# A graph network with attention and experts in one kernel: half PSUM tiles in a pool of their own, layer 2's alphas turned into one tile, and attention's first norms moved into the graph layers

## The chip, the cores and the metric

The kernel runs on one NeuronCore of a Trainium2 chip. A core has a matrix engine (TensorE, "PE" in the profile; its weight loads are "PEld"), a vector engine (VectorE, "DVE"), an activation engine (ScalarE, "ACT"), a general engine (GpSimd, "POOL") and a queue engine (SyncE, "SP") that here only issues DMAs. PE writes into PSUM, a memory of eight banks; DVE and ACT read it from there. Each engine works through its own list of instructions in order, and waits for other engines by semaphores. The metric is the device time of one execution in microseconds (us); lower is better.

## The reference

There are 625 nodes with 768 features and 20,000 edges, sorted by destination. All is float32. Cut to what matters:

```python
y = layernorm(x)
# two graph attention layers over the edges and the self loops
def gat(x, W, a_src, a_dst, bias, heads):
    xl = x @ W                                   # per head
    alpha_src, alpha_dst = xl . a_src, xl . a_dst
    e = leaky_relu(alpha_src[src] + alpha_dst[dst], 0.2)
    alpha = segment_softmax(e, dst)
    return segment_sum(xl[src] * alpha, dst) + bias
h1 = relu(layer_norm(gat(y, W1, ..., heads=4)) * g1 + be1) + (y @ Wr1 + br1)     # 1024 wide
h  = layer_norm(gat(h1, W2, ..., heads=1)) * g2 + be2 + (h1 @ Wr2 + br2)         # 768 wide
x = x + h
# one transformer block on layernorm(x): 12 heads, causal; then 8 experts, top 1
z = layernorm(x);  n = layernorm(z) * ln1_g + ln1_b
q, k, v = n @ Wq, n @ Wk, n @ Wv
u = z + causal_attention(q, k, v) @ Wp + bp
m = layernorm(u) * ln2_g + ln2_b
e = argmax(m @ Wg)
x = x + u + relu(m @ W1[e] + b1[e]) @ W2[e] + b2[e]
```

## The kernel before

The nodes are cut into five tiles of 125 rows (`T = 5`, `R = 125`), and most of the work is done tile by tile. The kernel has four stages.

**Counts (0 to about 129 us).** The edges become a dense matrix `C` of counts (destination by source) with one-hot matmuls. The counts gather in the PSUM tile `cps`, which is five banks wide (pool `cps`); projections and transposes use three more banks (pool `pps`, tag `p1`). `decode` turns `cps` into `C` with ACT and DVE. A branch follows (`tc.If(ok == 0)`, L445) whose body, rarely run, counts again in `cps`. All engines pass the branch.

**Graph layers (about 129 to 381 us).** A `Messages` object holds a tile's weights: `neg` marks missing edges, `weigh` makes the softmax weights `z` of a head (ACT adds the alphas, L170; DVE the leaky part, L171; DVE the maximum, L490; ACT the exponential, L493; DVE multiplies by `C`, L494), `turn` transposes `z` on PE, and `gather` multiplies it by `xl` into `agg`. PSUM comes from one pool, `gps`, with three tags: `half` (one bank, two buffers; from `psum_half`), `p2` (two banks, two buffers) and `acc` (two banks, one buffer). Halves take the projections and residuals: `project_residual` (L162) and `project` (L577) in layer 1, `second_residual` (L613) in layer 2. Its results are added to `x` on DVE (L615).

At the passage to layer 2, the alphas of the source nodes (`al2`) are turned to rows: for each tile a half tile, a transpose on PE (L624) and a copy on ACT (L625). Then `weigh2` makes the weights of the first three tiles; `messages2(t)` turns the next tile, weighs the one three ahead, gathers, adds the bias `br2` to `x` (L648), and `finish2` scales, normalises (L125 to L137) and adds to `x` (L640). The order on PE is written out by hand in these layers (`tc.manual_schedule`); on DVE and ACT a scheduler places instructions by its own estimates, and `tc.issue_after` holds one behind another. ACT works with tables of functions: going from a square root to an exponential or back takes a table load.

**Attention (about 381 to 640 us).** For each tile, the first norms are made: `bn_stats` (L735), mean and variance into `norms` (L736), two square roots on ACT (L738, L739), a reciprocal (L740), and `h` (L743, L745), which PE transposes (L715) into `hT`. `h` has two buffers. `hT` feeds the projections V (L759), Q and K (L796). `ln1_g` and `ln1_b` come by DMAs from POOL's queue (`load_v`, L685). The heads follow, two at a time.

**Experts (about 640 us to the end).** Rows are sorted to experts and worked off in blocks; expert weights (`ew`) stream in through SP's queue.

SBUF tiles come from pools whose addresses are taken over by later pools, so a tile also waits for the last reader of whatever lay at its place.

Of the kernel before, what the change touches and what calls it, by code (L numbers as in the profile page):

```python
# [9 lines left out]
F32 = mybir.dt.float32  # L10
# [4 lines left out]
AF = mybir.ActivationFunctionType  # L15
OP = mybir.AluOpType
AX = mybir.AxisListType
PSUM = bass.MemoryType.PSUM
DRAM = bass.MemoryType.DRAM

N = 625
R = 125
T = N // R
XR = 120
D = 768
KD = D // 128
# [15 lines left out]
B = 128  # L42
# [14 lines left out]
def row_bcast(v, n):  # L57

    return bass.AP(tensor=v.tensor, offset=v.offset, ap=[[0, B], [1, n]])
# [3 lines left out]
def gnn_moe_kernel(ctx: ExitStack, tc: tile.TileContext, p, out):  # L63
    nc = tc.nc
# [3 lines left out]
    keep = ctx.enter_context(tc.tile_pool(name="keep", bufs=1))  # L68
    small = ctx.enter_context(tc.tile_pool(name="small", bufs=4))
# [8 lines left out]
    x = xid[:, :, :D]  # L78
# [25 lines left out]
    eps = const.tile([128, 1], F32, name="eps")  # L104
# [14 lines left out]
    idr = ident[:R, :R]  # L119
# [14 lines left out]
    def norm_affine(o, a, n, g, b):  # L134
        mu, rs = norm_stats(a, n)
        nc.vector.scalar_tensor_tensor(o, a, mu, g, op0=OP.subtract, op1=OP.mult)
        nc.vector.scalar_tensor_tensor(o, o, rs, b, op0=OP.mult, op1=OP.add)  # L137

    def cols(t):
        return slice(t * R, (t + 1) * R)  # L140


    with tc.tile_pool(name="gnn", bufs=1) as gp:
        C = gp.tile([R, T, N], F32, name="C")
# [30 lines left out]
        with tc.tile_pool(name="oneh", bufs=12) as op_, \  # L175
# [104 lines left out]
            for t in range(2, T):  # L280
                nc.vector.scalar_tensor_tensor(tl, pt0[:R, :G], float(t * R), tl, op0=OP.is_ge,
                                               op1=OP.add)
# [4 lines left out]
                                           dst, op0=OP.mult, op1=OP.add)  # L287
# [157 lines left out]
            with tc.If(ok == 0):  # L445
# [13 lines left out]
                for t in range(T):  # L459

                    nc.vector.tensor_add(C[:, t, cols(t)], C[:, t, cols(t)], idr)

        with tc.tile_pool(name="gw", bufs=2, reuse_waits="tile") as gw, \
                tc.tile_pool(name="gps", bufs=2, space=PSUM, reuse_waits="tile") as ps:

            def psum_half():
                return ps.tile([128, 512], F32, tag="half", name="ph")

            def turn(dst, src, k, t):

                tp = ps.tile([128, 8, 128], F32, tag="p2", name="tp")
                for i in range(k):
                    nc.tensor.transpose(tp[:, i, :R], src[:, i * 128:(i + 1) * 128], idr)
                nc.scalar.copy(dst[:, :, cols(t)], tp[:, :k, :R])

            class Messages:


                def __init__(self, t, heads):
                    self.t, self.heads = t, heads  # L480
                    self.neg = gw.tile([R, N], F32, name="neg")
                    nc.vector.tensor_scalar(self.neg, C[:, t, :], 0.0, NEG, op0=OP.is_equal,
                                            op1=OP.mult)
                    self.tot = small.tile([R, HEADS], F32, name="tot")
                    self.z, self.zT, self.agg = {}, {}, None

                def weigh(self, h, rows, al, z=None):
                    z = z if z is not None else lifted(rows, al, self.t, h)
                    m = small.tile([R, 2], F32, name="m")
                    nc.vector.tensor_tensor_reduce(z, z, self.neg, scale=1.0, scalar=-3.0e38,  # L490
                                                   op0=OP.add, op1=OP.max, accum_out=m[:, 0:1])
                    nc.vector.tensor_scalar_mul(m[:, 1:2], m[:, 0:1], -1.0)
                    nc.scalar.activation(z, z, AF.Exp, bias=m[:, 1:2])  # L493
                    nc.vector.scalar_tensor_tensor(z, z, 1.0, C[:, self.t, :], op0=OP.mult,  # L494
                                                   op1=OP.mult, accum_out=self.tot[:, h:h + 1])
                    self.z[h] = z

                def turn(self, h):
# [37 lines left out]
            msgs = {0: Messages(0, HEADS)}  # L536
# [49 lines left out]
            hw = [messages(0)]  # L586
# [13 lines left out]
                project(t - 1)  # L600
            turn(h1T, hw[T - 1], KH, T - 1)


            b2 = load_bc("bc2", p["L0_gnn_b2"], D)
            g2 = load_bc("bc3", p["L0_gnn_g2"], D)
# [13 lines left out]
            br2 = load_bc("bc1", p["L0_gnn_br2"], D)  # L619
            second_residual(0, (1,))  # L620
            rows2 = gp.tile([R, HEADS, N], F32, tag="rows", name="rows2")
            for t in range(T):
                tp = psum_half()
                nc.tensor.transpose(tp[:R, :R], al2[:, 0, t, 0:1].to_broadcast([R, R]), idr)  # L624
                nc.scalar.copy(rows2[:, 0, cols(t)], tp[:R, :R])  # L625

            def weigh2(t):
                msgs[t] = Messages(t, 1)
# [13 lines left out]
            def messages2(t):  # L642
                if t + 1 < T:
                    msgs[t + 1].turn(0)
                if t + 3 < T:
                    weigh2(t + 3)
                msgs[t].gather(0, [(0, 0, 384), (512, 384, 384)], xl2, "p2" if t % 2 else "acc")
                nc.vector.tensor_add(x[:, t, :], x[:, t, :], br2)  # L648
                finish2(t)

            for t in range(3):
# [16 lines left out]
    nblk = keep.tile([1, 1], I32, name="nblk")  # L668
    table = keep.tile([1, 4, NS + 1], I32, name="table")
    first = keep.tile([1, 1], I32, name="first")  # L670


    sx = ctx.enter_context(tc.tile_pool(name="sx", bufs=1, side="right", reuse_waits="tile"))
    xa = sx.tile([B, D], F32, name="xa")
    xaT = sx.tile([128, KD, B], F32, name="xaT")
    ra = sx.tile([B, D + 1], F32, name="ra")
    pool, SP, PE = mybir.EngineType.Pool, mybir.EngineType.SP, mybir.EngineType.PE
    rt = ctx.enter_context(ExitStack())
    ap = rt.enter_context(tc.tile_pool(name="rt", bufs=1, side="right", reuse_waits="tile"))
    with tc.tile_pool(name="att", bufs=1, reuse_waits="tile") as a1, \  # L680
            tc.tile_pool(name="aw", bufs=3, reuse_waits="tile") as aw, \
            tc.tile_pool(name="aps", bufs=2, space=PSUM, reuse_waits="tile") as ps:

        def load_v(b, v):
            nc.gpsimd.dma_start(b, row_bcast(v, D))  # L685
            return b[:R]

        l1 = a1.tile([B, 2, D], F32, tag="aT", name="l1")
        l1g = load_v(l1[:, 0, :], p["L0_ffn_ln1_g"])
        l1b = load_v(l1[:, 1, :], p["L0_ffn_ln1_b"])  # L690
        bp, l2g, l2b = (load_v(ap.tile([B, D], F32, tag=n, name=n), p["L0_ffn_" + m])
                        for n, m in (("bp", "bp"), ("l2g", "ln2_g"), ("l2b", "ln2_b")))
        wg = ap.tile([128, KD, E], F32, name="wg")
        nc.gpsimd.dma_start(wg, p["L0_ffn_Wg"].rearrange("(k p) e -> p k e", p=128))
# [27 lines left out]

        norms = a1.tile([R, T, 4], F32, name="norms")

        def normed(t):
            nc.vector.tensor_scalar(xx[:, t, :], x[:, t, :], norms[:, t, 0:1], norms[:, t, 2:3],
                                    op0=OP.subtract, op1=OP.mult)
            nc.vector.tensor_add(xx[:, t, :], xx[:, t, :], bp)  # L730

        for t in range(T):
            st = small.tile([R, 2, 6], F32, name="st")
            for i in range(2):
                nc.vector.bn_stats(st[:, i, :], x[:, t, i * (D // 2):(i + 1) * (D // 2)])  # L735
            nc.vector.bn_aggr(norms[:, t, 0:2], st.rearrange("p a b -> p (a b)"))  # L736
            var = norms[:, t, 1:2]
            nc.scalar.activation(norms[:, t, 2:3], var, AF.Sqrt, bias=eps[:R])  # L738
            nc.scalar.activation(norms[:, t, 3:4], var, AF.Sqrt, bias=eps2[:R], scale=1.0 + EPS)  # L739
            nc.vector.reciprocal(norms[:, t, 2:4], norms[:, t, 2:4])  # L740
            hw = aw.tile([R, 2, N], F32, tag="e", name="h", bufs=2)
            hw = hw.rearrange("p h n -> p (h n)")[:, :D]
            nc.vector.scalar_tensor_tensor(hw, x[:, t, :], norms[:, t, 0:1], l1g, op0=OP.subtract,  # L743
                                           op1=OP.mult)
            nc.vector.scalar_tensor_tensor(hw, hw, norms[:, t, 3:4], l1b, op0=OP.mult, op1=OP.add)  # L745
            turn(hT, hw, KD, t)


        later = a1.tile([R, N], F32, name="later")
# [622 lines left out]
```

## Time and profile before

| | us |
|---|---|
| median of 3 runs | 1089.40 |
| the runs | 1086.68, 1089.40, 1089.96 |
| profiled execution, its own time | 1088.95 |
| its span, first to last instruction | 1086.4 |
| PE busy | 1012.5 (93% of the span) |
| DVE busy | 450.8 (41%) |
| ACT busy | 318.8 (29%) |
| POOL busy | 57.9 (5%) |
| mean granted PE clock | 0.978 of full |

The profiled execution is one of its own; sums made from its rows are compared with its own time, and that lies 0.45 us below the median. An engine's idle time is only lost if the end waits for it. Of an idle time, the view says what ended it; of a chain or a wait for several things, it names the one that came last.

### The profile page before, as it was taken

The numbers are of one execution on the slowest core, as the hardware profiler recorded it, in microseconds if no ns is written. First come the engines' busy times: TensorE is split into PE (matmuls) and PEld (weight loads), VectorE is DVE, ScalarE is ACT, GpSimd is POOL, SyncE is SP. The second block draws the span as 40 slices with busy tenths as digits, with TensorE's granted clock in tenths as the row PEclk, the third lists the DMA queues.
The fourth block names the chain that finished last, engine by engine and source line by source line (L and its number), as shares of the span: only waits on it lengthen the run. The fifth ranks groups of instructions, "written<-read, shape, count | busy, mean of one in ns | idle before, by whom it ended". The sixth has DMA issues, their size and how long they took to land. (4 is left out here: it accounts for less than half of the span.)

```text
span 1086.4 us, 14453 instructions
## 1 busy us (share of the span) xinstructions
PE 1012.5 (93%) x4763; PEld 578.2 (53%) x4764; DVE 450.8 (41%) x1264; ACT 318.8 (29%) x820; POOL 57.9 (5%) x97
## 2 busy tenths in 40 slices
PE   6889799999989989999999999999999889998993
PEld 4455366677555556666765655544454435533341
DVE  6796776385174740465546655011101121011211
ACT  6677534362140020344443401110201112021120
POOL 1200100000000100000000111000000000000000
PEclk9999899999999999999999999999999899998997
DMA  9300400300430164999200759111799948899694
GB/s 287 121 1 1 157 1 0 131 1 19 102 97 1 51 125 80 404 377 342 76 1 3 288 176 373 59 46 37 274 325 381 403 179 325 297 406 403 244 405 159
DMA packets 85669, 194.48 MB, mean 179 GB/s; under 512 B 32397, under 2 KB 34068, under 8 KB 85609
## 3 DMA queue, kind: packets, MB, share of 16 engines
q1 hardware_dynamic: 79817, 174.00, 44.9%
q0 software_dynamic: 5712, 19.54, 5.1%
q8 instruction: 36, 0.59, 0.2%
q10 hardware_dynamic: 80, 0.16, 0.1%
q14 instruction: 24, 0.20, 0.1%
HBM read 251.98 MB, written 38.37 MB: 267 GB/s over the span
## 5 line engine op out<-in xcount | busy, mean ns | idle before, releaser
L1102 PE MATMUL py<-ew,hbT 128*64 128x384 f32 (+2 forms) x960 | 194.4, 512 | 16.2 <-DMA ew<-in_L_ffn_W_dram 16.0
L1079 PE MATMUL ph<-ew,xbT 128*32 128x256 f32 (+2 forms) x864 | 155.6, 501 | 8.4 <-issue 4.8
L1102 PEld LDWEIGHTS py<-ew,hbT 128*64 128x64 f32 (+2 forms) x960 | 91.3, 149 | 101.0 <-issue 65.5
L1095 ACT ACTIVATE hbT<-tph,bT 128x64 f32<-128x64 f32 (+2 forms) x240 | 55.4, 333 | 267.4 <-PE tph L1090 166.2
L1079 PEld LDWEIGHTS ph<-ew,xbT 128*32 128x32 f32 (+2 forms) x864 | 64.8, 136 | 88.6 <-issue 81.7
L1154 DVE TENSOR_TENSOR yo<-yo,py 64x384 f32<-64x384 f32 (+2 forms) x40 | 23.0, 608 | 184.3 <-PE py L1102 183.9
L1083 DVE COPY hb<-ph 128x512 f32<-128x512 f32 (+1 forms) x39 | 24.4, 629 | 152.1 <-PE ph L1079 152.1
L515 PE MATMUL agg<-xl,zT 125*125 125x256 f32 (+1 forms) x300 | 79.8, 417 | 1.4 <-ACT zT L504 1.3
L515 PEld LDWEIGHTS agg<-xl,zT 125*125 125x125 f32 x300 | 54.5, 188 | 19.7 <-ACT zT L504 2.8
L227 ACT ACTIVATE step<-iota,past 125x314 f16<-125x314 f16 x120 | 55.9, 549 | 0.0
L352 PE MATMUL pp<-w,yT 128*125 128x512 f32 x120 | 55.3, 600 | 0.0
L613 PE MATMUL ph<-wr,h1T 128*125 128x384 f32 x160 | 54.5, 498 | 0.0
L577 PE MATMUL ph<-w,h1T 128*125 128x384 f32 x160 | 52.4, 486 | 0.0
L162 PE MATMUL ph<-wr,yT 128*125 128x512 f32 x96 | 44.4, 621 | 5.9 <-DVEq L445 5.9
L825 ACT ACTIVATE e<-e,nm 125x125 f32<-125x125 f32 (+4 forms) x60 | 36.0, 602 | 39.3 <-DVE nm L822 39.3
L244 PE MATMUL cps<-step,oh 125*125 125x314 f16 x181 | 37.1, 307 | 10.5 <-ACT step L227 7.4
L888 PE MATMUL po<-wpj,aT 128*125 128x384 f32 x120 | 44.3, 499 | 1.2 <-DVE nm L822 0.7
L237 DVE TENSOR_SCALAR oh<-iota,drel,upper 125x125 f16<-125x125 f16 x160 | 41.0, 313 | 3.2 <-PE cps L244 3.1
L613 PEld LDWEIGHTS ph<-wr,h1T 128*125 128x125 f32 x160 | 30.6, 193 | 21.6 <-issue 1.7
L577 PEld LDWEIGHTS ph<-w,h1T 128*125 128x125 f32 x160 | 30.0, 188 | 21.1 <-issue 0.5
L796 PE MATMUL pq<-hT,L_ffn_Wq 128*128 128x313 f32 (+1 forms) x144 | 41.0, 432 | 0.0
L822 DVE CUSTOM_DVE_ANT_0 e<-sc,later 125x125 f32<-125x125 f32 (+4 forms) x60 | 30.7, 543 | 24.0 <-PE sc L816 23.8
(326 smaller groups left out, 1252.3 us busy)
## 6 DMA issues: line engine op xcount, KB each, us to landing
ew<-in_L_ffn_W_dram SPq DMA_DIRECT2D x132, 1536.0 KB
xr<-zt SPq DMA_DIRECT2D x5, 3076.0 KB
xg<-zt SPq DMA_DIRECT2D x5, 3072.0 KB
w<-in_L_gnn_W_dram SPq DMA_DIRECT2D x4, 1536.0 KB
wr<-in_L_gnn_Wr_dram SPq DMA_DIRECT2D x4, 1536.0 KB
b2b<-in_L_ffn_b_dram SPq DMA_DIRECT2D x11, 384.0 KB
xb<-xg POOLq DMA_DIRECT2D x10, 384.0 KB, 6.4
rb<-xr POOLq DMA_DIRECT2D x9, 384.5 KB, 7.1
```

What stands on the lines that cost most here:

```text
L162: nc.tensor.matmul(pp[:R, :], yT[:, c, cols(t)], part(wr1, KD, c, i, 512), start=(c == 0), stop=(c == KD - 1))
L227: nc.scalar.activation(o, iota[:, :SH + 1], AF.Sign, bias=at, scale=-1.0)
L237: m = nc.vector.tensor_scalar(o, iota[:, :n], at, weight, op0=OP.is_equal, op1=OP.mult)
L352: nc.tensor.matmul(pp[:R, :], yT[:, c, cols(t)], part(w1, KD, c, i, 512), start=(c == 0), stop=(c == KD - 1))
L515: nc.tensor.matmul(self.agg[:R, c0:c0 + n], zT[:, s, :], xl[:, s, x0:x0 + n], start=(s == 0), stop=(s == T - 1))
L577: nc.tensor.matmul(ph[:R, :384], h1T[:, c, cols(t)], part(w2, KH, c, i, 384), start=(c == 0), stop=(c == KH - 1))
L613: nc.tensor.matmul(ph[:R, :384], h1T[:, k, cols(t)], part(wr2, KH, k, i, 384), start=(k == 0), stop=(k == KH - 1))
L796: nc.tensor.matmul(pp[:, :b - a], w[:, c, c0:c0 + 128], hT[:, c, a:b], start=(c == 0), stop=(c == KD - 1))
L888: mm = nc.tensor.matmul(pp[:R, i, :384], aT[:, c, cols(t)], wpj[i][:, c, :], start=(c == 0), stop=(c == KD - 1))
L1079: mm = nc.tensor.matmul(ph[g * M:(g + 1) * M, :C], xT[:, k, :M], w[:, k, o + g * C:o + (g + 1) * C], start=(k == 0), stop=(k == KD - 1))
L1095: nc.scalar.activation(hbT[c][:, k, r], tp[:, k, r], AF.Relu, bias=bT[:, f:f + 1])
L1102: mm = nc.tensor.matmul(py[g * M:(g + 1) * M, i, :384], hbT[c][:, k, g * M:(g + 1) * M], w[:, o + g * K + k, i * 384:(i + 1) * 384], start ...
```

## The change

- The half tiles get a PSUM pool of their own, `hps`, of two banks, opened after `gps`; `gps` keeps `p2` and `acc`.
- `neg` has one buffer instead of two.
- One exponential of a scratch value is put behind the last square root of layer 1.
- The five transposes of layer 2's alphas go into one tile of tag `p2`, and one ACT copy takes them out.
- The addition of `br2` is held behind the tile's own weights (`issue_after`).
- `ln1_g` and `ln1_b` are loaded at the start of the graph layers, into the tiles that later hold `xa` and `ra`; `norms` moves to the pool `keep`.
- The first norms of tiles 0 to 3 are scheduled with high priority (`tc.high_priority`); that of tile 4 is not.

Because pools and tags changed, tiles of attention lie at other addresses, such as `later`, `v`, `wpj0`, `wpj1` and `aT`.

```diff
+    def load_vector(b, v):
+        nc.gpsimd.dma_start(b, row_bcast(v, D))
+        return b[:R]
...
+        sx = ctx.enter_context(tc.tile_pool(name="sx", bufs=1, side="right", reuse_waits="tile"))
+        l1g = load_vector(sx.tile([B, D], F32, tag="xa", name="l1g"), p["L0_ffn_ln1_g"])
+        l1b = load_vector(sx.tile([B, D + 1], F32, tag="ra", name="l1b")[:, :D], p["L0_ffn_ln1_b"])
+        norms = keep.tile([R, T, 4], F32, name="norms")
         with tc.tile_pool(name="gw", bufs=2, reuse_waits="tile") as gw, \
-                tc.tile_pool(name="gps", bufs=2, space=PSUM, reuse_waits="tile") as ps:
+                tc.tile_pool(name="gps", bufs=2, space=PSUM, reuse_waits="tile") as ps, \
+                tc.tile_pool(name="hps", bufs=2, space=PSUM, reuse_waits="tile") as hps:
 
             def psum_half():
-                return ps.tile([128, 512], F32, tag="half", name="ph")
+                return hps.tile([128, 512], F32, name="ph")
...
-                    self.neg = gw.tile([R, N], F32, name="neg")
+                    self.neg = gw.tile([R, N], F32, name="neg", bufs=1)
...
-                    nc.vector.scalar_tensor_tensor(z, z, 1.0, C[:, self.t, :], op0=OP.mult,
-                                                   op1=OP.mult, accum_out=self.tot[:, h:h + 1])
+                    self.weighed = nc.vector.scalar_tensor_tensor(
+                        z, z, 1.0, C[:, self.t, :], op0=OP.mult, op1=OP.mult,
+                        accum_out=self.tot[:, h:h + 1])
...
             turn(h1T, hw[T - 1], KH, T - 1)
 
+            nc.scalar.activation(small.tile([R, 1], F32, name="sd"), eps[:R], AF.Exp)
...
+            tp = ps.tile([128, 8, 128], F32, tag="p2", name="tpa")
             for t in range(T):
-                tp = psum_half()
-                nc.tensor.transpose(tp[:R, :R], al2[:, 0, t, 0:1].to_broadcast([R, R]), idr)
-                nc.scalar.copy(rows2[:, 0, cols(t)], tp[:R, :R])
+                nc.tensor.transpose(tp[:R, t, :R], al2[:, 0, t, 0:1].to_broadcast([R, R]), idr)
+            nc.scalar.copy(rows2[:, 0, :].rearrange("r (t n) -> r t n", t=T), tp[:R, :T, :R])
...
-                nc.vector.tensor_add(x[:, t, :], x[:, t, :], br2)
+                with tc.issue_after(msgs[t].weighed.ins):
+                    nc.vector.tensor_add(x[:, t, :], x[:, t, :], br2)
...
-        l1 = a1.tile([B, 2, D], F32, tag="aT", name="l1")
-        l1g = load_v(l1[:, 0, :], p["L0_ffn_ln1_g"])
-        l1b = load_v(l1[:, 1, :], p["L0_ffn_ln1_b"])
...
-        for t in range(T):
-            st = small.tile([R, 2, 6], F32, name="st")
+        def first_norm(t):
+            st = small.tile([R, 2, 6], F32, name="st1")
...
             nc.vector.scalar_tensor_tensor(hw, hw, norms[:, t, 3:4], l1b, op0=OP.mult, op1=OP.add)
+            return hw
+
+        for t in range(T):
+
+            with tc.high_priority() if t < T - 1 else nullcontext():
+                hw = first_norm(t)
             turn(hT, hw, KD, t)
+        xa = sx.tile([B, D], F32, tag="xa", name="xa")
+        ra = sx.tile([B, D + 1], F32, tag="ra", name="ra")
```

More of the change, by code (lines that the diff above doesn't have):

```diff
@@ L670, in gnn_moe_kernel @@
     first = keep.tile([1, 1], I32, name="first")
[L673 to L676, printed above, removed]
+    sxt = ctx.enter_context(tc.tile_pool(name="sxt", bufs=1, side="right", reuse_waits="tile"))
+    xaT = sxt.tile([128, KD, B], F32, name="xaT")
     pool, SP, PE = mybir.EngineType.Pool, mybir.EngineType.SP, mybir.EngineType.PE
@@ L682, in gnn_moe_kernel @@
             tc.tile_pool(name="aps", bufs=2, space=PSUM, reuse_waits="tile") as ps:
-        def load_v(b, v):
-            nc.gpsimd.dma_start(b, row_bcast(v, D))
-            return b[:R]
-        l1 = a1.tile([B, 2, D], F32, tag="aT", name="l1")
-        l1g = load_v(l1[:, 0, :], p["L0_ffn_ln1_g"])
-        l1b = load_v(l1[:, 1, :], p["L0_ffn_ln1_b"])
-        bp, l2g, l2b = (load_v(ap.tile([B, D], F32, tag=n, name=n), p["L0_ffn_" + m])
+        bp, l2g, l2b = (load_vector(ap.tile([B, D], F32, tag=n, name=n), p["L0_ffn_" + m])
                         for n, m in (("bp", "bp"), ("l2g", "ln2_g"), ("l2b", "ln2_b")))
@@ L721, in gnn_moe_kernel @@
         hT = ap.tile([128, KD, N], F32, tag="xT", name="hT")
-        norms = a1.tile([R, T, 4], F32, name="norms")
         def normed(t):
```

## The prediction

> **What bounds the kernel now.** I read the page's busy shares first:
>
> ```profile
> PE 1012.5 (93%) x4763; PEld 578.2 (53%) x4764; DVE 450.8 (41%) x1264; ACT 318.8 (29%) x820; POOL 57.9 (5%) x97
> ```
>
> TensorE (PE) works for 93% of the span, so only time in which PE stands still, or runs at a lower clock, can be won. The change touches the graph layers and the start of attention, so I asked next what PE waited for between 120 and 400 us (columns: us in total, times, longest):
>
> ```profile
> PE ph L162 <- DVEq L445: 5.9, 1, 5.9
> PE tp L715 <- DVE h L745: 2.8, 1, 2.8
> PE ph L624 <- DVE xid L615: 2.5, 1, 2.5
> PE tpz L502 <- DVE z L494: 1.5, 1, 1.5
> PE agg L515 <- ACT zT L504: 1.3, 5, 0.3
> PE ph L624 <- ACT rows L625: 0.6, 2, 0.4
> ```
>
> Those are 14.6 us in 280 us; apart from them PE is full there, and from 400 to 640 us it waits under 2 us in all. So PE's order is a clock: what is taken out of a stop before 400 us moves everything behind it. The stops cost more than their length; busy time by stretch (span and length, PE busy, then the granted clock):
>
> ```profile
> 129.50:134.70 5.20, 5.16 (x7) 0.52 0.01 2
> 134.70:142.30 7.60, 7.60 (x19) 1.00 0.00 0
> 300.90:308.10 7.20, 7.17 (x17) 0.76 0.67 192
> ```
>
> After the stop of 5.85 us PE runs at half clock for 5.2 us, after the stops at 297 to 301 us at 0.76 for 7.2 us. The timeline shows the three places (start, duration; in brackets the idle time and what ended it):
>
> ```profile
> 129.54 13.00 PE L162 MATMUL ph<-wr,yT 128*125 128x512 f32 x24 [5.85 <-DVEq L445]
> 142.37 1.25 PE L502 MATMUL tpz<-ident,z 125*125 125x125 f32 x10
> ...
> 296.58 0.27 PE L624 MATMUL ph<-ident,al 125*125 125x125 f32 x1
> 298.58 0.96 DVE L648 TENSOR_TENSOR xid<-xid,bc 125x768 f32<-125x768 f32 x1 [4.61 <-DMA bc<-in_L_gnn_br_dram]
> 300.06 0.48 PE L624 MATMUL ph<-ident,al 125*125 125x125 f32 x2 [2.49 <-DVE xid L615]
> 304.45 1.28 ACT L493 ACT_TABLE_LOAD   x1
> 309.54 0.78 PE L502 MATMUL tpz<-ident,z 125*125 125x125 f32 x5 [1.47 <-DVE z L494]
> ...
> 383.71 1.51 PE L715 MATMUL tp<-ident,h 125*128 125x125 f32 x6 [2.83 <-DVE h L745]
> ```
>
> Place 1: the first residual halves (L162) wait for VectorE (DVE) to leave the branch at L445. Place 2: the alphas of layer 2 (L624) wait for a half tile that DVE frees late, since L648 ahead of it on DVE waits for a DMA. Place 3: attention's first transposes wait for the first norms.
>
> [...] it even slows after 2.8 us (0.89 mean over 381 to 396 us), but not after the 1.47 us at 309.54. [...]
>
> **Part 1, half tiles in their own pool (`hps`).** In the built program the halves move from PSUM banks 0 and 1, under the counts tile `cps` (banks 0 to 4) that the branch may rewrite, to banks 6 and 7, once of the projections. The first half then waits only for the ACT copy L373 at 118.04. PE's last matmul before the branch ends at 123.7; two halves' matmuls now stand ahead of the branch, and PE still passes it alone. I take 124.9 for the rest: 22 x 0.43 us (24 took 10.46 us at full clock at 153.68) = 9.5 us, end 134.4. Turn 0 of tile 0 then waits for its weights on DVE. DVE leaves the branch at 129.79 as before; of its queue, one `neg` (0.48) goes behind the four maxima (L490) and the first bias add L545 (0.69) comes ahead of the first L494, so that L494 starts at 134.45 instead of 134.21 and PE turns at 135.4 instead of 142.37: **7.0 us**. Next is late: DVE, whose L171 of tile 1 starts at 138.5 instead of 144.55, 6.0 earlier. It has some 2.8 us of idle a tile (1.46 before 164.19, 1.34 before 166.21) and some 20 us at 187 to 208, so it follows. Bounds: 3.9 if PE resumes later and cold (6 matmuls x 0.43 more), 7.0 is DVE's limit, 0 if PE is held at the join after all.
>
> `neg` with one buffer instead of two: written and read on DVE alone, in order; nothing.
>
> **Part 2, layer 2's alphas in one tile.** Five transposes go into one two-bank tile, last copied out at 277, so none waits for DVE: 296.58 to 297.3 (five at 309.54 took 0.78). One copy replaces five, 0.68 us (as zT's, 125x625), to 298.0. `br2`'s add (L648) now stands behind each tile's weights, so L615 runs at 296.9. Residual 1's first half: 16 x 0.328 = 5.25, 297.3 to 302.55, instead of 300.99 to 308.07. Weights of tile 0: z on ACT at 298.0, L171 0.85 behind it, L490 at 300.3 (1.45 on), two L171 and `neg` between, exponential at 302.0 (no load ahead), L494 at 302.95, turn at 303.95 (0.96 behind, as before) instead of 309.54: **5.6 us**. PE stops 1.4 us there, as before, so without a cold clock. Tile 1's weights: L490, L615, `neg`, L648 and L490 of tile 2 stand before its L494, which ends at 308.7; PE turns it at 309.8, so it just fits. DVE reaches tile 0's finish near 319.5 instead of 317, and catches up in the 5 us of idle it has in each 17 us. Bounds 4.5 to 6.5.
>
> The early exponential behind the last root of layer 1 costs ACT 1.28 + 0.2 us from 268.4, in the 1.74 us that ACT then idles before L579 at 270.12: nothing. It takes the load at 304.45 away, counted above.
>
> **Part 3, the first norms.** Statistics of tiles 0 to 3 (2 x 0.55 + 0.2 + 0.15 = 1.5 us each) move into DVE's idle time behind each L640. But `h` has two buffers, the second over `be2` (bc0), which finish 4 reads last. DVE's built order, on the old clock: aggregate 4 at 370.6; L637 x2, statistics and affine with tile 3's leftovers to 375.6; `h` of tiles 0 and 1 (4 x 0.93) to 379.2; L640 0.95, memset 0.58, L615 x2 1.1, memset 0.7, L735 0.5: 382.7. Then `h` of 2 is ready at 386.15, of 3 at 387.0, of 4 at 390.4 (behind a 0.56 copy of v). PE ends its residual at 380.9 and does not stop for `h` 0: 12 transposes (with their copies, 2.0) and 5 matmuls of V (1.6) last to 384.5, then it waits 1.7; tile 2, one matmul, tile 3, two, to 388.9; waits 1.5; tile 4 to 391.2. Only 8 of 120 V matmuls are done, 20 before. The other 112 x 0.323 = 36.2 end at 427.4; before 427.5. **0.1 us**: the stop in front turns into two stops inside. Bounds: +4 (the 2.8 and the cold clock behind it) if DVE is earlier, -3 if the two stops halve the clock.
>
> The loads of `l1g`, `l1b` move ahead of `a_src2`, `b2`, `g2`, `be2`, `br2` on POOL's queue, 2 x 0.54 us; they need only the buffers freed at the branch, and POOL then idles until 198.61: nothing. `later`'s select (1.42) with its wait for DVE near 380 comes ahead of the loads of `bp`, `l2g`, `l2b`, `wg` (2.5 to issue, 6.1 to land), so these land near 390 instead of 366, with `bp` first used after 445: nothing. SP keeps its order; `wpj0` now lies over `xl2` and waits for the last aggregate (370) instead of issuing at 299.55; the Wq load behind it waits until 378.33 anyway.
>
> **Sum.** 7.0 + 5.6 + 0.1 = 12.7 us. Attention and the experts see the same order and work, 12.7 us earlier. The profiled execution took 1088.95 us (span 1086.4), so 1076.25; it lies 0.45 below the median shown, 1089.40, so **1076.7 us**.
>
> **Rivals.** A: as worked out, own range 1074 to 1079; chance 0.60. B: the third part pays in full, because DVE has its statistics done and reaches `h` of 2 earlier; for it, DVE idles 5 us per tile there; against it, the order above. 12.6 + 4 gives 1072.8; 0.13. C: one of the first two does not hold: PE stays at the join of L445 (the branch names all engines), or the weights of layer 2 refill the place. Left are 5.7 or 7.1, 1083.7 or 1082.3; 0.17. D: everything before 640 us is earlier, but the experts' stage starts with loads whose buffers moved (the first, `ew0_1`, now waits for PE and DVE), and these pace it. In favour: PE waits 16.0 us for `ew` there and the chain that ended last holds 6% of DMA. If they start as late as now, no change (0.05). If they start later than 641.85 by more than 3.3 us, each further us is lost and the kernel is slower; 5 us gives 1094 (0.05). Against: these buffers are freed by attention's last matmuls, which move with PE.
>
> **Numbers.** About 0.3% (3.3 us) is what a measurement of this kernel can tell from no change. Faster: A, B, C, 0.90; same 0.05; slower 0.05. The range takes A, B and the nearer half of C, and the runs' own spread (3.3 us between three): 1072 to 1083.
>
> **What would show it.** Right: no wait of L162's halves for the branch, clock near 1 at 125 to 140; the turn of layer 2's tile 0 about 12.6 earlier than 309.54; no stop before the first `h` transposes, but two of 1 to 2 us before the third and fifth; V's end about 12.7 before 427.5. Wrong: PE idle to 129.5; PE waiting for L494 of tile 1; the first expert's loads not earlier than 641.85.

## The result, and the profile after

| | before | after |
|---|---|---|
| median | 1089.68 us (4 runs) | 1071.24 us (4 runs: 1070.25, 1070.60, 1071.89, 1073.72) |
| ratio | | 0.9832, 95% interval 0.9811 to 0.9854 |
| profiled execution, its span | 1088.95, 1086.4 us | 1070.60, 1067.9 us |

The change makes the kernel some 18 us faster, between 15.9 and 20.6 by the interval; 12.7 were forecast, and the median lies 0.8 us below the range. Two further sets of runs of the changed kernel have medians of 1072.66 and 1072.71; over all its 13 runs the median is 1072.3.

Busy time by engine, kernel after:

```profile
PE 1006.7 (94%) x4763; PEld 574.8 (54%) x4764; DVE 451.7 (42%) x1264; ACT 319.0 (30%) x817; POOL 57.1 (5%) x97
```

PE works off the same 4763 rows of matmuls in 5.8 us less, because fewer of them run at a low clock (its mean is 0.985 of full, before 0.978). The other 12.7 us of the span are stops that went; that this is the number of the forecast is chance, since stops from the whole kernel are in it. PE's waits between 120 and 430 us, kernel after (us in total, times, longest):

```profile
PE tpz L515 <- DVE z L506: 2.5, 2, 1.5
PE agg L528 <- ACT zT L517: 1.1, 4, 0.3
PE tp L720 <- DVE h L749: 0.5, 2, 0.3
PE tp L720 <- ACT hT L722: 0.3, 1, 0.3
```

14.6 us have become 4.4. PE's timeline at the three places, kernel after (start, duration; in brackets the idle time and what ended it):

```profile
123.79 10.85 PE L166 MATMUL ph<-wr,yT 128*125 128x512 f32 x24
135.71 1.45 PE L515 MATMUL tpz<-ident,z 125*125 125x125 f32 x10 [1.08 <-DVE z L506]
...
289.98 0.71 PE L639 MATMUL tpa<-ident,al 125*125 125x125 f32 x5
297.31 0.78 PE L515 MATMUL tpz<-ident,z 125*125 125x125 f32 x5 [1.47 <-DVE z L506]
...
368.50 0.81 PE L720 MATMUL tp<-ident,h 125*128 125x125 f32 x6
370.93 2.75 PE L771 MATMUL pv<-L_ffn_Wv,hT 128*125 128x384 f32 x8
373.94 0.83 PE L720 MATMUL tp<-ident,h 125*128 125x125 f32 x6 [0.26 <-DVE h L749]
377.56 0.83 PE L720 MATMUL tp<-ident,h 125*128 125x125 f32 x6 [0.21 <-DVE h L749]
378.22 33.71 PE L771 MATMUL pv<-L_ffn_Wv,hT 128*125 128x384 f32 x104
411.77 6.48 PE L808 MATMUL pq<-hT,L_ffn_Wq 128*128 128x313 f32 x24
```

Place 1: the halves run straight on from the projections, with no bracket. Place 2: five alphas in one go. Place 3: no bracket at 368.50, and two small ones where the prediction expected 1.7 and 1.5 us. The clock in the first two places, kernel after (stretch and length, PE busy, granted clock, DMA share, GB/s):

```profile
123.70:129.50 5.80, 5.65 (x14) 1.00 0.02 6
129.50:135.70 6.20, 5.13 (x12) 1.00 0.40 130
289.90:297.30 7.40, 5.95 (x22) 1.00 0.68 160
```

It stays at 1.00, where before it fell to 0.52 and 0.76. So the 18.5 us between the two spans divide like this (starts in us; the first two of before are in the prediction's views, the next two in the lines below):

| up to | before | after | gained there |
|---|---|---|---|
| turn of layer 1's tile 0 | 142.37 | 135.71 | 6.66 |
| turn of layer 2's tile 0 | 309.54 | 297.31 | 12.23 - 6.66 = 5.57 |
| Q's first matmul | 427.50 | 411.77 | 15.73 - 12.23 = 3.50 |
| first expert's first product | 642.32 | 627.93 | -1.34 |
| end of the span | 1086.4 | 1067.9 | 4.11 |

The loss of 1.34 us in the fourth row has a place. SP's, POOL's and PE's timelines, kernel before first:

```profile
427.50 6.48 PE L796 MATMUL pq<-hT,L_ffn_Wq 128*128 128x313 f32 x24
...
633.50 0.61 POOL L1005 DMA_DIRECT2D xa<-xg  x1 [4.35 <-DMA xg<-h,pos]
...
637.03 0.87 PE L879 MATMUL tpx<-ident,xa 128*128 128x128 f32 x6
...
641.31 0.35 SPq L1031 DMA_DIRECT2D b2b<-in_L_ffn_b_dram  x1
...
642.32 10.57 PE L1079 MATMUL ph<-ew,xaT 128*128 128x512 f32 x24 [0.49 <-DVE xx L896]
```

Kernel after:

```profile
617.28 0.34 SPq L1043 DMA_DIRECT2D b2b<-in_L_ffn_b_dram  x1
...
617.80 0.61 POOL L1017 DMA_DIRECT2D xa<-xg  x1 [4.30 <-DMA xg<-h,pos]
...
622.63 0.88 PE L891 MATMUL tpx<-ident,xa 128*128 128x128 f32 x6 [1.19 <-DMA xa<-xg]
627.93 10.57 PE L1091 MATMUL ph<-ew,xaT 128*128 128x512 f32 x24 [0.49 <-DVE xx L908]
```

The first expert's bias (`b2b`) used to be sent at 641.31, when attention's output projection had read `aT`, whose place it takes. The third part moved attention's buffers; `b2b` now takes the place of `later`, free earlier, and its 384 KB go out half a microsecond ahead of the rows `xa`. These land in 4.8 us instead of 3.5, and PE waits for them.

In the last row PE is busy for as long as before (404.7 and 404.6 us), so the 4.11 us are waits that went (27.0 us before, 23.0 after). 3.2 of them are waits for the experts' weights (us in total, times, longest), kernels before and after:

```profile
PE py L1102 <- DMA ew<-in_L_ffn_W_dram: 16.0, 7, 3.1
```

```profile
PE py L1114 <- DMA ew<-in_L_ffn_W_dram: 12.8, 7, 3.3
```

Why they became shorter was open.

### The profile page after: what moved, and what is told of

It is laid out like the page before. It is cut to its first block, busy times and chain, and to the rows that moved or that the text cites. A ratio compares the mean times of both kernels' runs of the same rounds, so it can differ in the third digit from the quotient of the medians.

```text
span 1067.9 us, 14435 instructions
## 1 busy us (share of the span) xinstructions
PE 1006.7 (94%) x4763; PEld 574.8 (54%) x4764; DVE 451.7 (42%) x1264; ACT 319.0 (30%) x817; POOL 57.1 (5%) x97
## 5 line engine op out<-in xcount | busy, mean ns | idle before, releaser
L166 PE MATMUL ph<-wr,yT 128*125 128x512 f32 x96 | 42.1, 593 | 0.1
```

The source lines that it names most:

```text
L166: nc.tensor.matmul(pp[:R, :], yT[:, c, cols(t)], part(wr1, KD, c, i, 512), start=(c == 0), stop=(c == KD - 1))
```

## The experiments

All starts are from each kernel's own profile, in us. "Up to Q" is from the turn of layer 2's tile 0 to Q's first matmul, "to experts" from there to the first expert's first product, "stage" from there to the end of the span. The ratio is to the kernel before in the same comparison.

| kernel | median (runs) | ratio, 95% interval | up to Q | to experts | stage |
|---|---|---|---|---|---|
| before | 1089.68 (4) | | 117.96 | 214.82 | 444.1 |
| after | 1071.24 (4) | 0.9832, 0.9811 to 0.9854 | 114.46 | 216.16 | 440.0 |
| half_pool | 1083.64 (8) | 0.9941, 0.9920 to 0.9962 | 118.43 | 214.73 | 444.2 |
| both_turns | 1076.93 (6) | 0.9883, 0.9862 to 0.9905 | 119.29 | 214.74 | 444.0 |
| first_norms | 1084.48 (22) | 0.9955, 0.9942 to 0.9968 | 114.45 | 216.18 | 439.7 |
| whole_again | 1072.66 (5) | 0.9839, 0.9814 to 0.9863 | 114.45 | 216.49 | 442.4 |
| v_behind | 1078.53 (4) | 0.9905, 0.9873 to 0.9937 | 123.27 | 216.59 | 440.6 |
| no_priority | 1070.97 (4) | 0.9840, 0.9804 to 0.9876 | 114.62 | 216.83 | 440.2 |
| old_places | 1071.65 (4) | 0.9844, 0.9817 to 0.9871 | 114.45 | 214.80 | 440.9 |
| whole_third | 1072.71 (4) | 0.9855, 0.9827 to 0.9883 | 114.45 | 216.69 | 442.4 |
| before_shifted | 1088.20 (14) | 0.9996, 0.9978 to 1.0014 | 117.94 | 214.97 | 440.7 |
| after_residues | 1073.18 (6) | 0.9860, 0.9834 to 0.9885 | 114.46 | 216.07 | 441.8 |
| aligned | 1067.91 (6) | 0.9819, 0.9788 to 0.9850 | 114.46 | 215.93 | 438.9 |
| old_places_aligned | 1066.65 (6) | 0.9803, 0.9778 to 0.9828 | 114.46 | 214.89 | 436.2 |
| norms_kept | 1074.57 (4) | 0.9862, 0.9829 to 0.9896 | 117.79 | 214.72 | 442.2 |
| two_tiles | 1071.02 (6) | 0.9828, 0.9801 to 0.9856 | 114.74 | 214.86 | 443.4 |
| two_tiles_aligned | 1069.17 (6) | 0.9815, 0.9788 to 0.9843 | 114.75 | 214.89 | 436.2 |
| before_aligned | 1085.69 (20) | 0.9968, 0.9955 to 0.9980 | 119.42 | 214.80 | 438.3 |

### One part at a time

**half_pool**, the first part alone:

```diff
-                tc.tile_pool(name="gps", bufs=2, space=PSUM, reuse_waits="tile") as ps:
+                tc.tile_pool(name="gps", bufs=2, space=PSUM, reuse_waits="tile") as ps, \
+                tc.tile_pool(name="hps", bufs=2, space=PSUM, reuse_waits="tile") as hps:
-                return ps.tile([128, 512], F32, tag="half", name="ph")
+                return hps.tile([128, 512], F32, name="ph")
```

> The kernel before with the first part alone: the half tiles get a pool of their own, nothing else is touched. My theory (each part pays in its own stage, and the gain in the experts' stage came with the buffers that the third part moved): TensorE goes through the branch without its stop, the turn of layer 1's tile 0 starts near 135.7 us instead of 142.37, and the kernel is faster by 6.7 us, at about 1083.0 us, with the experts' stage (from the first product of the first expert to the end) as long as before, 444.1 us. Rival (the experts' stage gained because it starts earlier, wherever its buffers lie): part of the 2.8 us that the whole change gained there shows here too, and the time is 1080 to 1082 us. Second rival (the first part hides behind DVE and returns before layer 2): no more than 2 us faster, 1087 to 1089 us.

Its turn starts at 137.06. The ratio makes it 6.4 us (4.1 to 8.7), the medians 5.9, the stage has its old length. The first part pays in its own place and keeps what it pays; the rival in which it hides behind DVE has fallen, and so has the one in which an earlier start shortens the experts' stage.

**both_turns**, the first two parts. Its diff is the change's, without the lines on `sx`, `norms`, `neg`, `first_norm` and `xa`.

> The kernel before with the first and second part, so the whole change without the early first norms and without the moved buffers. My theory: the turn of layer 2's tile 0 starts near 297.3 us, 12.2 us earlier than before, attention's first transposes stop as before, the experts' stage is as long as before, and the kernel takes 1089.7 - 12.2 = 1077.5 us. Then the third part and what comes with it are worth 1077.5 - 1071.2 = 6.3 us of the change, of which 3.5 up to Q's first matmul. Rival (the experts' stage gains by starting earlier): 1074.5 to 1076 us, and the third part is worth some 3.5 us only. The prediction's own working has 1077.1 us for this kernel, and 0.1 us for what is missing in it.

1076.93 against 1077.1 and 1077.5: both workings hold. The place that is left, PE's timeline, kernel both_turns:

```profile
371.68 1.51 PE L720 MATMUL tp<-ident,h 125*128 125x125 f32 x6 [2.82 <-DVE h L750]
...
416.79 6.47 PE L801 MATMUL pq<-hT,L_ffn_Wq 128*128 128x313 f32 x24
```

The stop of 2.82 us stands as before, and six transposes behind it take 1.51 instead of 0.81 us: the clock falls. The stage is 444.0. How long the clock stays low behind this stop differs: before and before_aligned have the same program up to Q and take 117.96 and 119.42 us there (the second tile's six transposes 1.03 and 1.46 us). The six kernels with the stop lie between 117.8 and 119.4 us.

**first_norms**, the third part alone:

```diff
+        l1g = load_vector(sx.tile([B, D], F32, tag="xa", name="l1g"), p["L0_ffn_ln1_g"])
+        l1b = load_vector(sx.tile([B, D + 1], F32, tag="ra", name="l1b")[:, :D], p["L0_ffn_ln1_b"])
+        norms = keep.tile([R, T, 4], F32, name="norms")
...
+            st = small.tile([R, 2, 6], F32, name="st1")
...
+            with tc.high_priority() if t < T - 1 else nullcontext():
+                hw = first_norm(t)
```

> The kernel before with the third part alone: vectors of the first norm loaded early, first norms at high priority, one buffer for neg, and the places of attention's buffers as after the change. My theory (the prediction counted the V matmuls between the transposes in instructions of the program where the trace has two rows for each, so that the cover was twice as large as it worked out): Q's first matmul starts 3.5 us earlier than before, near 424.0 us, the experts' stage is shorter by 2.8 us, and the kernel takes 1083.0 to 1083.8 us. The prediction's working: 0.1 us for the stage, 1089.6 us. Rival (third part pays only while DVE reaches the last tile early, thanks to the other two): 1 us or less up to Q.

The third part alone is worth 4.9 us (3.5 to 6.3), and 3.51 up to Q (117.96 to 114.45), without any help of the other two. Against the slowest kernel with the stop it would be 5.0 us. The 0.1 us of the prediction has fallen. 1 - 0.9883 and 1 - 0.9955 add up to 0.0162, and the whole has 0.0161:

> The whole change once more, beside its parts and on the same chip. If the parts add up without touching each other, its gain is that of the first two together plus that of the third alone, within 1 us, and its median lies near 1071.2 us with the experts' stage at about 440 us, 4.1 us less than the 444.1 before (1.2 us of it are the wait for xa that has been taken out of that stage's start). If the gain in the experts' stage was a chance of one profiled execution, this execution's stage is back near 443 us, and the time near 1073 us.

The parts add up. The stage took 442.4 us this time, and PE's wait for weights in it is 16.2 us, as long as before the change: 2.4 of the 4.1 us that the first profile showed can be the spread of one execution.

### Why the third part pays 3.5 and not 0.1 us

**v_behind** puts V's matmuls behind all first transposes on PE:

```diff
+        v_order = ExitStack()
+        v_order.enter_context(tc.manual_schedule(engines={mybir.EngineType.PE}))
         for t in range(T):
...
             turn(hT, hw, KD, t)
...
+        v_order.close()
```

> The whole change, but on TensorE all 30 transposes of the five first norms stand ahead of V's 60 matmuls (order of the program), instead of 8 V matmuls between them. My theory (those 8 matmuls are 16 rows of the trace at 0.324 us, 5.2 us of work that covers DVE's way to the third and the fifth h): TensorE stops again, in all some 5 us, ahead of the third to fifth tile's transposes, and Q's first matmul comes 5.2 us later than in the whole change, counted from the turn of layer 2's tile 0: 119.7 us instead of 114.5, more by up to 1 us if the clock falls after a stop. Time 1077 to 1079 us. The prediction's working (8 rows of 0.324 us): 2.6 us later, 117.1 us, time near 1075. Rival (third part pays through the early statistics and not through the cover): no change, 114.5 us and 1072.3 us.

PE's timeline, kernel v_behind, then the clock:

```profile
373.74 2.59 PE L720 MATMUL tp<-ident,h 125*128 125x125 f32 x12 [2.96 <-DVE h L749]
378.61 1.49 PE L720 MATMUL tp<-ident,h 125*128 125x125 f32 x6 [2.28 <-DVE h L749]
379.88 41.13 PE L773 MATMUL pv<-L_ffn_Wv,hT 128*125 128x384 f32 x120
```

```profile
373.70:380.00 6.30, 3.95 (x19) 0.54 1.01 264
380.00:388.00 8.00, 8.00 (x20) 0.72 0.67 194
```

Q comes 123.27 us behind the turn, later than the 119.7 expected. The stops have grown from 0.47 to 5.24 us, 4.8 more, as the cover of 16 rows (5.2 us) had it. The 2.6 us of the prediction's count could not give that. What nobody expected in this size is the clock: 120 rows of V, 38.9 us at 0.324, take 41.1, and the 18 transposes behind the two stops 4.1 instead of 2.5 us. Stops and clock make 8.6 of the 8.8 us that Q is later. The eight V matmuls in between save more than their own length, because they keep the stops at 0.26 and 0.21 us, behind which PE isn't slower in this trace.

**no_priority** takes the high priority away again (`hw = first_norm(t)` without the `with`).

> The whole change without the high priority of the first four first norms; the early load of the norm's vectors, the single buffer for neg and the moved buffers stay. My theory (the third part pays because DVE writes the first two h before the last residual's end): h of tile 0 is ready after the last addition of the residual again, TensorE stops some 2 us ahead of the first transposes, and from the turn of layer 2's tile 0 to Q's first matmul it takes 116.5 to 118 us, instead of 114.5 (118.0 in the kernel before, 119.3 with the first two parts). Time 1074.5 to 1076 us. Rival (early loaded vectors are what matters): 114.5 us, no change of time, 1072.3 us.

My theory of it was wrong: 114.62 us, no stop before the first transposes, 1070.97 us. The scheduler puts the norms early without being told to. Then what else lets it? Two runs took two buffers alone, over both_turns.

**norms_kept**, `norms` in the pool that lives through the kernel:

```diff
+        norms = keep.tile([R, T, 4], F32, name="norms")
...
-        norms = a1.tile([R, T, 4], F32, name="norms")
```

> The first two parts, and of the third only that the tile norms lies in the pool that lives through the whole kernel instead of in attention's pool. My theory (norms in attention's pool takes the place of a graph tile that is still in use, so its first writer is put behind that tile's last reader; the statistics' buffer st, shared with the graph layers' norms, does the same): with one of two holds left, the statistics of four tiles still stand between the last two layer norms on DVE, h of tiles 0 and 1 is ready after the residual's end, and from the turn of layer 2's tile 0 to Q's first matmul it takes 118 to 119.5 us; time 1076 to 1077.5 us. Rival (norms alone is the hold): 114.5 us and 1071.5 to 1073 us.

**two_tiles**, that and a buffer of its own for the statistics:

```diff
-            st = small.tile([R, 2, 6], F32, name="st")
+            st = small.tile([R, 2, 6], F32, name="st1")
```

> The first two parts, and of the third only two buffers: norms in the pool that lives through the whole kernel, and a buffer of its own for the statistics of the first norms (st1). No early load of the vectors, no high priority, one more buffer for neg than in the change, attention's buffers in the old order. My theory: that is all of the third part that works: statistics early, first two h ahead of the last additions, 114.5 to 114.8 us from the turn to Q's first matmul, and no stop ahead of xa's transposes, since the bias's load stays behind attention: time 1070.5 to 1072 us, no slower than the whole change. Rival (the early vectors are needed as well): 116 us or more up to Q, 1073.5 us or more.

norms_kept comes out a little under what was expected of it, 117.79 us up to Q and 1074.57 us; two_tiles is as expected. DVE's and PE's timelines, kernel norms_kept first:

```profile
370.17 0.54 DVE L620 TENSOR_TENSOR xid<-xid,ph 125x384 f32<-125x384 f32 x1
371.44 1.81 DVE L750 SCALAR_TENSOR_TENSOR h<-h,norms,l 125x768 f32<-125x768 f32 x2
...
372.39 1.22 PE L721 MATMUL tp<-ident,h 125*128 125x125 f32 x6 [2.62 <-DVE h L750]
```

Kernel two_tiles:

```profile
367.87 1.94 DVE L750 SCALAR_TENSOR_TENSOR h<-h,norms,l 125x768 f32<-125x768 f32 x2
369.73 0.55 DVE L620 TENSOR_TENSOR xid<-xid,ph 125x384 f32<-125x384 f32 x1
...
368.94 0.86 PE L721 MATMUL tp<-ident,h 125*128 125x125 f32 x6
```

With `norms` alone `h` (L750) still stands behind the last addition of the residual (L620), and PE stops 2.62 us. With both buffers the order is turned round and the stop is gone: 114.74 us up to Q. So two buffers are nearly all of the third part. The statistics' buffer alone was not run; that `norms` is needed as well is not shown. The likely reason is that a tile that lies in a later pool, or that shares its name with one still in use, ties its first writer to somebody else's last reader; the scheduler then has nothing to move. For `st` the traces fit it: in norms_kept the first statistics of attention (L740) run at 361.48, right behind the graph layers' last ones (L125, 360.56), in two_tiles at 317.29. The early vectors and the priority, and with them the moved places, add 0.3 us up to Q. That the vectors' early load does nothing could be seen before: in the old profile POOL sent them at 318 us, and `h` needed them at 379.65.

### The start of the experts' stage

**old_places** gives attention's buffers their old order by unused tiles:

```diff
+        a1.tile([B, 2, D], F32, tag="aT", name="kept")
+        a1.tile([R, T, 4], F32, name="kept_norms")
```

> The whole change with attention's buffers where they were before (an unused tile keeps the old order of places), the experts' tiles staying at the changed kernel's addresses. The load of the first expert's bias then lands on aT, which is read until attention's end, and not on the mask of the last query tile. Theory A (that load, sent early, stands in the way of xa's, and the experts' stage is not paced by its start): it is sent at attention's end again, xa's load lands in 3.5 instead of 4.8 us, the stop of 1.2 to 1.5 us ahead of xa's transposes goes, from Q's first matmul to the first expert's product it takes 214.8 instead of 216.2 us, the time falls by 1.3 us to about 1071.0 us. Theory B (the experts' stage is paced by its weights' loads, so that what the start loses or gains is made up there): the stop goes, the stage is longer by as much, 1072.3 us. Theory C (moved places are what made the experts' stage shorter): stage back at 444 us, the time rises by 1 to 2.8 us to 1073.5 to 1075 us.

> The whole change a third time, on the chip of the three kernels beside it, as their measure: from the turn of layer 2's tile 0 to Q's first matmul 114.5 us, a stop of 1.2 to 1.5 us ahead of xa's transposes, time 1070 to 1073.5 us with a median near 1072. If the experts' stage's length differs from run to run by chance, this profile shows again another one than 440.0 and 442.4 us; if the places set it, it is within 1 us of 440.

SP's and PE's timelines, kernel old_places:

```profile
625.73 0.34 SPq L1045 DMA_DIRECT2D b2b<-in_L_ffn_b_dram  x1
...
626.75 10.57 PE L1093 MATMUL ph<-ew,xaT 128*128 128x512 f32 x24 [0.49 <-DVE xx L910]
```

`b2b` goes out 8.4 us later, `xa` lands in 3.4 us, the stop is gone, and "to experts" is back at 214.80. That this cause made the stop is shown. What it is worth at the end is not: 1071.65 us, and whole_third beside it 1072.71 us, with intervals that overlap almost wholly. Theory C has fallen, since the stage stays at 440.9 with attention's old places. whole_third's stage is 442.4 us, where 439.0 to 441.0 would have spoken for a length that the places set: it differs between executions of one kernel.

### The length of the experts' stage

The third part also shifts the experts' weight tiles by 352 bytes. **before_shifted** does that alone, **after_residues** shifts the changed kernel's by 160 more, **aligned** puts all six at multiples of 512:

```diff
     ewa = ctx.enter_context(tc.tile_pool(name="ewa", bufs=1, reuse_waits="tile"))
+    ewa.tile([B, 88], F32, name="filler")       # before_shifted; 40 in after_residues, 64 in aligned
...
+    ewb.tile([B, 56], F32, name="filler2")      # aligned only
```

> The kernel before with an unused tile of 352 bytes ahead of the experts' tiles, so that these lie where the change puts them (first weight tiles 256 bytes past a multiple of 512 instead of 416, the later ones 32 instead of 192); nothing else is touched. Theory A (the place of the experts' weight tiles sets how fast their loads are written, and the third part moved them): in the two stretches where the loads run without a gap, 184 to 194 and 312 to 322 us after the first expert's first product, 416 to 422 GB/s instead of 408 to 415; the experts' stage takes 440 to 442.4 us instead of 444.1, and the time falls by some 2.2 us, to about 1087.3 us. Rival (something else in the third part, or the moment at which the stage starts): 408 to 415 GB/s, 444 us, no change of time.

> The whole change with an unused tile of 160 bytes ahead of the experts' tiles: they lie at other addresses than before, but as far past a multiple of 512 bytes as before (416 and 192). Theory A with residues as the reason: 408 to 415 GB/s in the two stretches, experts' stage back at about 443 to 444 us, time some 2.2 us up, to 1074.5 us. Rival (the residue is not what matters, or the rate is not set by the place): 416 to 422 GB/s and 1072.3 us.

> The whole change with two unused tiles, of 256 and 224 bytes, so that each of the experts' six weight tiles starts at a multiple of 512 bytes. Theory A with residues: the rate is at least that of the change, 420 GB/s or more, the experts' stage 438 to 441 us, time 1070 to 1072 us. Rival (place is nothing): 416 to 422 GB/s, stage 440 to 442.4 us, time 1072.3 us. If multiples of 512 were the worse case, 408 to 415 GB/s and 1074 us or more.

> The version meant to be the best: the whole change with attention's buffers in their old places (no stop ahead of xa's transposes) and the experts' weight tiles at multiples of 512 bytes. If both help on their own, 1069.5 to 1071 us, with 214.8 us from Q's first matmul to the first expert's product and an experts' stage of 439 to 441 us. If the stage is paced by its loads, the removed stop is made up for there and it equals the aligned version. If neither helps, 1072 us.

The first of the two stretches of loads (length, PE busy, clock, DMA share, GB/s), kernels before_shifted, after_residues and two_tiles, which has the changed kernel's addresses:

```profile
826.60:836.60 10.00, 10.00 (x50) 1.00 1.02 419
```

```profile
812.30:822.30 10.00, 10.00 (x56) 1.00 1.02 408
```

```profile
811.30:821.30 10.00, 10.00 (x56) 1.00 1.02 410
```

The first two are as theory A has them (before had 413, after 420). two_tiles isn't: 410 at addresses where after had 420. So the rate over 10 us is no clean measure of the place, and I use the stage's length and the time instead. before_shifted's stage is 3.4 us shorter, but its time is the same as before's (0.9996); the execution that was profiled took 1085.31 us, 2.9 less than the median of its runs, so its stage is not the usual one. after_residues' time, 1073.18, lies 0.9 us above the change's median, within the spread of runs. Neither settles the 352 bytes.

With multiples of 512 aligned has 1067.91 us and old_places_aligned 1066.65 us, both less than expected. But aligned's interval, 0.9788 to 0.9850, still overlaps with those of the changed kernel. Whether the places help other kernels was asked of the next two (the two fillers again: 608 and 224 bytes over before, 256 and 224 over two_tiles).

> The kernel before with the experts' six weight tiles at multiples of 512 bytes by two unused tiles, nothing else touched. Theory A (the place sets the loads' rate, and the loads hold up the experts' stage): experts' stage 437 to 441 us instead of 444.1, time 3 to 5 us less, 1085 to 1086.5 us. Rival (only kernels with the new first parts gain from it, or chance): within 1.5 us of before, 1088 to 1090 us.

> The kernel with two buffers as in two_tiles, and the experts' weight tiles at multiples of 512 bytes. If the places add to it as they did to the whole change (4.4 us in medians, with an experts' stage of 436 to 439 us): 1066 to 1067.5 us, the least of all, level with old_places_aligned. If the gain of the aligned kernels was chance: 1070.5 to 1072 us, as two_tiles.

before_aligned is faster than before by 3.5 us (2.2 to 4.9 by the interval, 20 and 25 runs). two_tiles_aligned misses its 1066 to 1067.5: 1069.17, with runs from 1064.8 to 1070.7; its profile has the short stage, but is that of its fastest run, as old_places_aligned's is too. PE's wait for the weights in it, against 16.0 us with stops of up to 3.1 before:

```profile
PE py L1108 <- DMA ew<-in_L_ffn_W_dram: 14.6, 7, 2.8
```

Sorted afterwards by how far past a multiple of 512 bytes the six weight tiles start, the stages are: as before, 416 and 192 bytes (before, half_pool, both_turns, after_residues), 441.8 to 444.2, mean 443.5; as in the change, 256 and 32 bytes (after and its two repeats, and the seven other kernels with a shifted start; norms_kept, one of them, has the first two at multiples and the other four not), 439.7 to 443.4, mean 441.2; all six at multiples (the four aligned kernels), 436.2 to 438.9, mean 437.4.

The profiles hold a rival to this. In 14 of the 18 PE stops once for 4.4 to 4.8 us ahead of an expert's products, with no cause that the trace shows, and the 96 rows behind the stop take 6.84 to 8.37 us. In first_norms, before_shifted, before_aligned and two_tiles_aligned this stop is missing. PE's timeline, kernels before and before_aligned:

```profile
857.22 7.57 PE L1079 MATMUL ph<-ew,xbT 128*32 128x256 f32 x96 [4.79 <-issue]
```

```profile
853.63 5.39 PE L1080 MATMUL ph<-ew,xbT 128*32 128x256 f32 x96
```

The addresses don't decide on it: the experts' weights lie at the same ones in the changed kernel and in first_norms. The order of the three groups stays when the kernels with the stop (443.5, 441.5 and 437.6 us) and those without it (440.2 and 437.2 us for the second and the third group) are taken by themselves. Without it the stage is shorter by 1.3 us at most: in first_norms and before_shifted PE waits 18.9 and 17.8 us for weights, in the kernels of their group with the stop 12.5 to 16.2. That speaks for a stage that is paced by its loads (theory B of old_places), but no run was made for it.

That these two fillers make the kernel before faster is shown by before_aligned's runs; that the multiple of 512 bytes is the reason rests on the sorting, since other tiles move with the weights. By what way a place would cost time is not shown. How much of the change's 4.11 us comes from the places of its weight tiles is not shown either. The means make it 2.3 us, or 2.0 among the kernels with the stop.

old_places_aligned, the change with old places for attention and aligned weights, has the lowest median, 1066.65 us, 0.9803 of before; its interval overlaps with those of aligned and two_tiles_aligned.

## Why the prediction was right or wrong

**What bounds the kernel: right.** All that was gained up to Q came out of PE's stops and the slow clock behind them.

**Part 1, 7.0 us: right**, 6.66. The halves end at 134.64 (134.4 forecast), the turn waits for DVE's weights as forecast and starts at 135.71 (135.4). PE passes the join alone; rival C has fallen for this part.

**Part 2, 5.6 us: right**, 5.57. The five transposes take 0.71 us, the residual's half starts in their wake, the stop ahead of the turn is 1.47 us, and the clock behind it holds at 1.00 (297.30 to 305.00). The exponential's early table load (L616, 1.28 us) shows in no wait of PE.

**Part 3, 0.1 us: wrong**, 3.50. The step that failed is "Only 8 of 120 V matmuls are done, 20 before. The other 112 x 0.323 = 36.2", and, before it, "5 matmuls of V (1.6)". V is 5 tiles x 2 halves x 6 matmuls, 60 in the program; the trace shows x120, two rows for each (a transpose has one: x6 for a tile), and 0.324 us is the time from one row to the next. The 8 and the 5 were read from the order of the program and multiplied by the price of a row, and taken off 120, which are rows, as the 20 before are. In the trace 10, 2 and 4 rows stand where the prediction has 5, 1 and 2 matmuls, and 104 rows are left behind the fifth `h`. v_behind shows what these 16 rows cover: without them the stops grow by 4.8 us. The rest of the working held: the third `h` was forecast 5.25 us behind the residual's end (380.9 to 386.15), and PE takes it 5.3 us behind (368.65 to 373.94); the fifth at 9.5, and PE has it at 8.9. With 8 more rows, 2.6 us, and the 0.6 us of the fifth `h`, the same working gives 3.3 us. (One sum is a little off, too: 379.2 and the six times behind it make 383.0, not 382.7; it moves no other number by more than that.) The parts 1 and 2 had used rows throughout (24 for a residual, 16 for a half), so they were not hit. "Bounds +4 to -3" held the value, but the reason given for +4 was an earlier DVE, and the third `h` came no earlier than forecast: that was luck.

**Rival B, "the third part pays in full", 1072.8 us,** was given 0.13. Its size nearly came, 3.5 of 4 us, but not its reason, since DVE did not reach `h` of 2 earlier. That its total lies within 1.6 us of the measured one is in part luck: the experts' stage is in the measurement and not in B.

**"Attention and the experts see the same order and work, 12.7 us earlier": wrong on both sides.** The list of moved loads named `wpj0` and the vectors; it left out `b2b`, whose place changed hands too and whose early load costs 1.34 us in front of the experts. This is rival D's mechanism, with another load and a fraction of its size; the first expert's loads themselves came at 626.91 instead of 641.85, as hoped. The 4.11 us behind it were foreseen by nobody: before_aligned's runs, 3.5 us faster by two fillers, show that the kernel can answer to where its tiles lie, not how much of the 4.11 is that.

**The range.** It ended at 1072.0, 4.7 us below the forecast, with nothing in it for the experts' stage, although its wait for weights of 16.0 us stood in the working of rival D and buffers there were known to have moved. Its lengths of 442.4, 442.4 and 440.0 us in three profiles of one kernel show the spread that a range has to hold. The median of all 13 runs, 1072.3, lies just inside the range; the step that failed in part 3 fails either way.

## What to carry to other kernels

Before a number of instructions is multiplied by a duration, make sure that both come from the same list; here one float32 matmul was two rows, and a cover worked out at 2.6 us was 5.2. When a scheduler doesn't move work that has all its inputs, look at the place and the name of what it writes: here two small buffers alone brought all but 0.3 us of what early loads and a priority were thought to bring. A change of buffers early in a kernel moves the addresses of all that follows; compare later stages as well, and ask which load now goes out first.

## What the runs showed of the hardware

- A stop's length alone doesn't tell whether PE slows behind it. In the experts' stage each kernel stops for DVE's `yo` once, and 24 products follow: behind 2.30 us in before and 2.00 in before_shifted they took 12.23 us (mean clock in before 0.86), behind 2.05 in half_pool, 2.06 in aligned and 1.90 in after 10.54 (in after 1.00). What decides between the two is not shown.
- A float32 matmul of 384 columns (V) is two rows in these traces, 0.324 us from one to the next; a float32 transpose of 125 columns is one.
- Two fillers that put the six weight tiles at multiples of 512 bytes, moving them and other tiles by less than 1 KB, made the kernel before 3.5 us faster (20 and 25 runs). The stage that loads them was 5.8 us shorter in its profile, but that profile lacks the stop of 4.79 us as well.
